# Eight node blocks instead of seven summed along gathered rows in each propagation step of a GNN kernel, with their stores issued by ScalarE

## The chip, the core and the metric

The kernel runs on one NeuronCore of a Trainium2 chip. Its engines are named as in the profile: PE (TensorE; PEld is its weight load), DVE (VectorE), ACT (ScalarE), POOL (GpSimd) and SP (SyncE, which only issues DMAs here). The metric is the device time of one execution in microseconds (us); lower is better. Each engine takes its instructions from its own queue in program order, and waits at the head of the queue for the semaphores that the next instruction names.

## The reference

Four graph layers act on 6250 nodes with 128 features (float32) and 100,000 edges that are sorted by destination. L0 is a mean over neighbours with two dense maps, a spectral filter, batch normalisation and GELU; L1 a relational convolution with 32 relations; L2 an attention layer with a feed-forward block. Before each, the nodes are layer-normalised, and each adds its result to `x`. The layer that matters here is the last one, ten steps of propagation over the same graph with self loops:

```python
src = jnp.concatenate([src, loop]); dst = jnp.concatenate([dst, loop])
norm = deg_inv_sqrt[src] * deg_inv_sqrt[dst]
def step(xk, _):
    msg = norm[:, None] * xk[src]
    agg = jax.ops.segment_sum(msg, dst, num_segments=n_nodes)
    return ((1.0 - ALPHA) * agg + ALPHA * h, None)
xK, _ = jax.lax.scan(step, x, None, length=K)          # K = 10
return jax.nn.relu(xK)
```

## The kernel before

The nodes are padded to 49 blocks of 128. With `z` the state scaled by the root of the degree, a step of L3 is a plain sum over neighbours, followed by one multiply and one add per node. The kernel gets that sum in two ways.

**By products.** For blocks 0 to `DW - 1` (42 of them) the adjacency matrix lies in DRAM as counts in fp8 (`adj`, built in L0 and L1 by `counted` and `put_matrix`; the self loop is put in too). `z` is kept in SBUF as two parts, a high and a low one, in `parts[step % 2]` (tiles `xr0` and `xr1`, type fp32r). A *group* is up to four destination blocks (`GD`): ten groups of four and one of two. A group's columns run over the 49 source blocks in *pieces* of seven source blocks (`GS`); the group of two has four pieces. A step so has 74 pieces (`NP`), and a piece goes through four hands:

- `load` (L1680): SP issues the DMA of the fp8 counts into `am` (six buffers).
- `cast` (L1691 on ACT, L1689 on DVE): the counts become fp32r in `ar` (three buffers). Every third piece is cast by DVE, the others by ACT. Piece n can be cast when piece n-3 is through PE.
- `product` (L1701, in two halves): for each source block and each part one matmul with the 128x128 part as weights and 512 columns of `ar` moving (256 in the group of two), summed in one PSUM bank.
- at a group's end `evict` (L1707, ACT) copies the sums to SBUF as `y`, `turn_back` (L1712, PE) transposes them, and `rows_behind` makes the new state: `scale` on DVE (L1626, L1631, L1632), `keep` on ACT (L1640, the high part), `store` on POOL (L1644, the new `z` to the table `z_at` in DRAM).

**By gathered rows.** For the last seven blocks (42 to 48) the edges are cut into 128 lanes of `LE` = 114 consecutive edges. `collect` has POOL gather, with one indirect DMA per list place (L694), the 128 rows of `z_at` that the lanes need at this place, `LC` = 6 places to a tile `rows3` (four buffers). `run_on` (L1003, DVE) adds along each lane, restarting where the destination changes; its first instruction reads the last row of the tile before. `put_down` (L1008) stores the running sums in the table `scan`; the lane ends go to `carried` (L1007). There are 19 such rounds in a step. Then `fetch_ends` gathers, for each of the seven blocks, a node's sum from `scan` and what the lane before it carried over, loads the node's own `z` row (`own`, through SP), and `add_up` (L1725, L1726, DVE) adds the three. `rows_behind` follows for these seven blocks too (`kind` "t", tail).

**The order.** All of this is put in one list, `plan`, with a time for each entry, in units of one piece; sorting it by time gives every engine's queue, and nothing is reordered afterwards. The last lines set it:

```python
pace, behind, late = 2.75, 6.2, 2
...
tiles, n = {}, step * NP + behind
for k in range(LE // LC):
    there = n + pace * (k + 1)
    then(there - pace, collect, rp, end3, k, z_at[step % 2], LC, tiles, "rows3")
    there = slot(there + late)
    then(there, run_on, end3, k, LC, tiles)
    there += 1.6
    then(there, put_down, nc.gpsimd.dma_start, end3, k, LC, tiles)
```

`slot` rounds a time up to the next multiple of three pieces (plus 0.01), which is just behind a cast of DVE's. So `scale` and `run_on` stand in DVE's queue behind such a cast, and `put_down` 1.6 pieces later in the queue of the engine that issues it. The steps follow each other without a barrier. A step first works on groups 0 and 1 over source blocks 0 to 34, because the last blocks of the state before come late.

Of the kernel before, what the change touches and what calls it, by code (L numbers as in the profile page):

```python
# [10 lines left out]
F32 = mybir.dt.float32  # L11
# [4 lines left out]
OP = mybir.AluOpType  # L16
# [5 lines left out]
D = 128  # L22
E = 100000
P = 125
# [49 lines left out]
F32R = mybir.dt.float32r  # L74
F8 = mybir.dt.float8e4
MULTI = 15
GD = 4
GS = 7
DW = 42
DW0 = 36  # L80
LE = 114
LE0 = 216
LC = 6
LC0 = 8
# [554 lines left out]
def _fast(ctx, tc, a, out, pre):  # L639
    nc = tc.nc  # L640
    TT, TS, STT = nc.vector.tensor_tensor, nc.vector.tensor_scalar, nc.vector.scalar_tensor_tensor
    ident, eps, deg = pre["ident"], pre["eps"], pre["deg"]
    P, W = FP, FW
# [16 lines left out]
    def nodes(table):  # L660
        return table.rearrange("(w p) d -> p w d", p=P)
# [53 lines left out]
    def list_end(name, w0, le):  # L715

        n = W - w0
        return dict(w0=w0, le=le, e0=E - LP * le, n=n, name=name,
                    src=const.tile([LP, le], I32, name=f"src_{name}"),
                    same=const.tile([LP, le], F32, name=f"same_{name}"),  # L720
                    end=const.tile([P, n], I32, name=f"end_{name}"),
                    carry=const.tile([P, n], I32, name=f"carry_{name}"),
                    scan=dram.tile([LP * le + 1, D], F32, name=f"scan_{name}"),
                    carried=dram.tile([LP + 1, D], F32, name=f"carried_{name}"))

    end0, end3 = list_end("e0", DW0, LE0), list_end("e3", DW, LE)

# [8 lines left out]
    z_at = [dram.tile([FN, D], F32, name=f"z_at{i}") for i in range(2)]  # L736
    z_first = dram.tile([FN, D], F32, name="z_first")
    h_rows = dram.tile([FN, D], F32, name="h_rows")

    adj = dram.tile([DW, P, W * P], F8, name="adj")  # L740

# [6 lines left out]
    late = l1_lists.enter_context(tc.tile_pool(name="flate1", bufs=1, side="right"))  # L748
# [13 lines left out]
    late = lists.enter_context(tc.tile_pool(name="flate", bufs=1))  # L762
# [12 lines left out]
                   allow_small_or_imprecise_dtypes=True)  # L775
    lane_sum = keyp.tile([CH, DW * GW // 4], F32, name="lane_sum")
    key_v = keyp.tile([CH, GB * 128], BF16, name="key_v")
# [13 lines left out]
    with tc.tile_pool(name="csr_k", bufs=1) as sp, tc.tile_pool(name="csr_kps", bufs=2, space=PSUM) as pp2:  # L791
# [9 lines left out]
        got = sp.tile([128, GB, CH], I32, name="p_got")  # L801
# [25 lines left out]
        for b0 in range(0, GB, 4):  # L827
            n = min(4, GB - b0)
# [218 lines left out]
    with tc.tile_pool(name="bxs", bufs=1) as bx, tc.tile_pool(name="bps", bufs=2, space=PSUM) as bps, \  # L1047
# [78 lines left out]
        tiles = {}  # L1126
# [20 lines left out]
        behind = None  # L1147
        for w in range(DW0 + 1):
# [15 lines left out]
            if w < DW0:  # L1164
                put_matrix(w, stag, bst)
                behind = stag
# [17 lines left out]
    with tc.tile_pool(name="fl1w", bufs=2) as wp, tc.tile_pool(name="fl1hr", bufs=3) as hp, \  # L1184
# [23 lines left out]
        def matrix_rest():  # L1208
            for w in range(DW0, DW):
                stag = bst.tile([P, W, P], F8, name="stag1")  # L1210
# [102 lines left out]
    own = l2p.tile([P, W, H], F32, name="own")  # L1313
# [9 lines left out]
    with tc.tile_pool(name="fl2w", bufs=2) as wp, tc.tile_pool(name="fl2ps", bufs=2, space=PSUM) as pp:  # L1323
# [5 lines left out]
        got, ht2 = {}, {}  # L1329
# [43 lines left out]
    with tc.tile_pool(name="fl2d", bufs=1) as l2d, tc.tile_pool(name="fl2r", bufs=4) as rp, \  # L1373
# [68 lines left out]
        state = None, None  # L1442
        for i in range(NT - FIRST, NT):
            rows = fetched(i)
            state = run(i, rows, *state)
# [11 lines left out]
        state = begin[:, SW:], begin[:, :SW]  # L1457
        for i in range(NT - FIRST):
            rows = fetched(i)
            state = run(i, rows, *state)  # L1460
# [8 lines left out]
        more = l2d.tile([LP, SW], F32, name="more2")  # L1469
# [14 lines left out]
    parts = [last.enter_context(tc.tile_pool(name="fl3x0", bufs=1)).tile([P, W, 2, D], F32R, name="xr0")]  # L1484
    with tc.tile_pool(name="fl2f", bufs=2) as fp, tc.tile_pool(name="fl2fps", bufs=1, space=PSUM) as pp, \
# [5 lines left out]
        got, fac, h1, ht3, ffs, us, z0 = ({} for _ in range(7))  # L1491
# [77 lines left out]
        def part5(b):  # L1569
# [23 lines left out]
    ap, cp, yp, sp, rp, ep = (last.enter_context(tc.tile_pool(name=f"fl3{k}", bufs=n))  # L1593
                              for k, n in (("a", 6), ("c", 3), ("y", 1), ("s", 2), ("r", 4), ("e", 1)))
# [7 lines left out]
    def then(time, do, *args):  # L1602
        plan.append((time, len(plan), do, args))

    def slot(time):

        return 3 * -int(-time // 3) + 0.01

    def rows_behind(time, step, w0, n, at):

        out_at, kind = step == K_STEPS - 1, "t" if w0 == DW else ""
        pool, wide = (ep, end3["n"]) if kind else (sp, GD)
        z_to, new = z_at[(step + 1) % 2], parts[(step + 1) % 2][:, w0:w0 + n]

        def fetch():
            at["first"] = pool.tile([P, wide, D], F32, name=f"first3{kind}")[:, :n, :]
            nc.sync.dma_start(at["first"], nodes(z_first)[:, w0:w0 + n, :])

        def fetch_kept():
            at["t"] = at["own"] if kind else pool.tile([P, wide, D], F32, name="split_t")[:, :n, :]  # L1620
            nc.sync.dma_start(at["t"], nodes(x_kept)[:, w0:w0 + n, :])

        def scale():
            z = at["z"] = at["more"] if kind else pool.tile([P, wide, D], F32, name="z3")[:, :n, :]
            for i in range(n):
                STT(z[:, i, :], at["sums"][:, i, :], d9[:, w0 + i:w0 + i + 1], at["first"][:, i, :],  # L1626
                    op0=OP.mult, op1=OP.add)
            if out_at:
                return
            at["t"] = at["own"] if kind else pool.tile([P, wide, D], F32, name="split_t")[:, :n, :]  # L1630
            TS(at["t"].bitcast(I32), z.bitcast(I32), -4096, None, op0=OP.bitwise_and)  # L1631
            TT(new[:, :, 1, :], z, at["t"], OP.subtract)  # L1632

        def keep():
            if out_at:
                for i in range(n):
                    nc.scalar.activation(at["z"][:, i, :], at["z"][:, i, :], AF.Relu,  # L1637
                                         scale=back[:, w0 + i:w0 + i + 1])
            else:
                nc.scalar.copy(new[:, :, 0, :], at["t"])  # L1640

        def store():
            if not out_at:
                nc.gpsimd.dma_start(nodes(z_to)[:, w0:w0 + n, :], at["z"])  # L1644
                return
            xb = at["t"]
            TT(xb, xb, at["z"], OP.add)  # L1647
            m = min(n, full - w0)
            nc.sync.dma_start(nodes(out[0:full * P, :])[:, w0:w0 + m, :], xb[:, :m, :])
            if m < n:  # L1650
                nc.sync.dma_start(out[full * P:N, :], xb[:tail, m, :])

        then(time - 6, fetch)
        if out_at and not kind:
            then(time - 1, fetch_kept)
        time = slot(time)
        then(time, scale)
        if out_at and kind:
            then(time + 0.05, fetch_kept)
        then(time + 2.3, keep)  # L1660
        then(slot(time + 2.4) if out_at else time + 2.7, store)

    groups = [(w, min(GD, DW - w)) for w in range(0, DW, GD)]
    cuts = [[W * i // n for i in range(n + 1)] for n in (W * nd // (GS * GD) + (W * nd % (GS * GD) > 0) for _, nd in groups)]
# [3 lines left out]
    loads, casts, sums = {}, {}, {}  # L1670
# [43 lines left out]
    def fetch_ends(step, at):  # L1714

        n = end3["n"]
        at["got"], at["more"], at["own"] = (ep.tile([P, n, D], F32, name=f"{k}3") for k in ("got", "more", "own"))
        nc.sync.dma_start(at["own"], nodes(z_at[step % 2])[:, DW:, :])
        for i in range(n):
            gather(at["more"][:, i, :], end3["carried"], end3["carry"], i)  # L1720
        for i in range(n):
            gather(at["got"][:, i, :], end3["scan"], end3["end"], i)

    def add_up(at):
        TT(at["more"], at["own"], at["more"], OP.add)  # L1725
        TT(at["got"], at["got"], at["more"], OP.add)  # L1726
        at["sums"] = at["got"]

    pace, behind, late = 2.75, 6.2, 2
    for step in range(K_STEPS):  # L1730
        for at, (g, c) in enumerate(order):
            n, key = step * NP + at, (step, g, c)
            then(n - 6.3, load, key)
            then(n - 2, cast, key, n)
            then(n, product, key, False)
            then(n + 0.45, product, key, True)
            if c == len(cuts[g]) - 2:
                state = {}
                then(n + 1, evict, g, state)
                then(n + 1.4, turn_back, g, state)  # L1740
                rows_behind(n + 1.75, step, *groups[g], state)
# [4 lines that stand above are left out]
            there = slot(there + late)  # L1746
            then(there, run_on, end3, k, LC, tiles)
            there += 1.6
            then(there, put_down, nc.gpsimd.dma_start, end3, k, LC, tiles)
        state = {}  # L1750
        then(there + 0.1, fetch_ends, step, state)
        there = slot(there + 6)
        then(there, add_up, state)
        rows_behind(there - 0.5, step, DW, end3["n"], state)
    with tc.manual_schedule():
        for _, _, do, args in sorted(plan, key=lambda p: p[:2]):
# [5 lines left out]
def gnn4_kernel(ctx: ExitStack, tc: tile.TileContext, a: dict, out: bass.AP):  # L1762
# [21 lines left out]
    with tc.tile_pool(name="csr", bufs=1) as sp, tc.tile_pool(name="csr2", bufs=4) as sp2, \  # L1784
# [89 lines left out]
        least = sp.tile([FW, 1], F32, name="p_least")  # L1874
        nc.gpsimd.memset(least, float(E - LP * LE) - 0.5)
        for w, e0 in ((DW, E - LP * LE0 - 0.5), (DW0, -1.0)):
# [72 lines left out]
```

## Time and profile before

| | us |
|---|---|
| median of three runs | 6846.81 (6821.8 to 6847.55) |
| the profiled execution's own time | 6823.96 |
| its span from first to last instruction | 6822.2 |
| L3, from the first product to the last | 3993 to 6808 |
| PE, DVE, ACT, POOL busy over the span | 3676.2, 3345.3, 2747.3, 3537.3 |
| PE, DVE, ACT, POOL busy in a mean step of L3 (of 281.5) | 252.6, 159.4, 167.6, 143.3 |

How to read it: the profile comes from one execution, so durations and sums are held against 6823.96. A PE record has its start and a modelled end, so matmuls overlap in it, and the distance between two starts says how fast PE is going. Gaps on an engine are put down to what released it. L3 is the stretch in which the change acts almost alone; its ten steps are counted from the last product of one to the last product of the next.

### The profile page before, as it was taken

To read this page: it belongs to the slowest core of one execution; us is meant where nothing else is said; L and a number is where in the kernel's file an instruction comes from. 1 tells how busy PE (TensorE), PEld (TensorE's weight loads), DVE (VectorE), ACT (ScalarE), POOL (GpSimd) and SP (SyncE) were. 2 spreads that over 40 slices of the span, in tenths; PEclk is the share of its full clock that TensorE was granted. 3 is DMA by queue.
4 is the path that set the end of the run, shared out by engine and by line. 5 is a ranking of instruction groups with operands and counts; after the bars stand their busy time and mean duration, and the time that the engine had idled before them with its cause. 6 is when DMAs were issued, how large, how long until landed. Compare 5 with 4: busy or idle time off the path is not lost. (4 is left out here: it accounts for less than half of the span.)

```text
span 6822.2 us, 55524 instructions
## 1 busy us (share of the span) xinstructions
PE 3676.2 (54%) x16892; PEld 2753.4 (40%) x16892; DVE 3345.3 (49%) x7571; ACT 2747.3 (40%) x3219; POOL 3537.3 (52%) x3583
## 2 busy tenths in 40 slices
PE   3655999700000020000000478799898998989998
PEld 3533654300000010000000157677776777767776
DVE  7454655422222224444545655556555565645655
ACT  0333655432222220000000565566565665656665
POOL 1265000177777756677676425446454554554644
PEclk8577999855555555555555799899998999989998
DMA  2233136632222213232222257677676776767766
GB/s 67 73 115 106 66 137 290 261 114 97 90 96 92 94 57 103 94 101 90 98 91 98 79 159 211 178 206 227 185 214 180 207 218 188 212 180 203 224 196 191
DMA packets 692861, 1003.89 MB, mean 147 GB/s; under 512 B 95753, under 2 KB 590738, under 8 KB 673094
## 3 DMA queue, kind: packets, MB, share of 16 engines
q1 hardware_dynamic: 546720, 677.59, 30.4%
q0 software_dynamic: 128304, 318.10, 16.1%
q10 hardware_dynamic: 17526, 4.56, 0.3%
q8 instruction: 134, 2.20, 0.1%
q14 instruction: 177, 1.45, 0.1%
HBM read 605.13 MB, written 397.87 MB: 147 GB/s over the span
## 5 line engine op out<-in xcount | busy, mean ns | idle before, releaser
L1701 PE MATMUL dense<-ar,xr 128*128 128x512 f32 (+1 forms) x10780 | 2495.7, 392 | 207.7 <-ACT ar L1691 89.1
L1701 PEld LDWEIGHTS dense<-ar,xr 128*128 128x128 f32 x10780 | 2015.0, 195 | 644.0 <-issue 124.5
L1691 ACT CAST ar<-am 128x3584 fp32r<-128x3584 fp8e4 (+1 forms) x494 | 1560.4, 3169 | 964.4 <-issue 385.3
L1689 DVE CAST ar<-am 128x3584 fp32r<-128x3584 fp8e4 (+1 forms) x246 | 933.8, 3796 | 1162.0 <-PE dense L1701 630.0
L694 POOL DMA_INDIRECT rows<-z_at,src_e x1140 | 1093.0, 959 | 667.5 <-issue 388.4
L694 POOL DMA_INDIRECT rows<-ftable,lane_src x782 | 833.2, 1065 | 366.0 <-issue 239.9
L694 POOL DMA_INDIRECT rows<-ftable,rel_l x782 | 830.4, 1062 | 245.2 <-issue 236.2
L1534 PE MATMUL ht_ps<-ident_p,h1g 128*128 128x128 f32 x49 | 10.3, 298 | 1270.4 <-ACT h1g L684 1270.1
L702 PE MATMUL ht_ps<-ident_p,long 128*128 128x128 f32 x49 | 16.0, 442 | 1129.3 <-ACT long L684 1125.8
L1282 ACT ACTIVATE rows<-rows,lane_norm 128x128 f32<-128x128 f32 x782 | 312.3, 401 | 766.3 <-issue 609.7
L1284 DVE SCALAR_TENSOR_TENSOR rows<-rows,same 128x128 f32<-128x128 f32 x733 | 257.8, 352 | 724.8 <-ACT rows L1282 610.4
L1534 PEld LDWEIGHTS ht_ps<-ident_p,h1g 128*128 128x128 f32 x49 | 6.6, 144 | 1279.9 <-ACT h1g L684 1275.2
L702 PEld LDWEIGHTS ht_ps<-ident_p,long 128*128 128x128 f32 x49 | 10.0, 208 | 1134.7 <-ACT long L684 1128.5
L1003 DVE SCALAR_TENSOR_TENSOR rows<-rows,same_e 128x128 f32<-128x128 f32 x1139 | 401.4, 352 | 44.4 <-issue 3.9
L1032 ACT ACTIVATE stag<-cnt_ps 128x784 fp8e4<-128x784 f32 x336 | 276.0, 823 | 340.5 <-remote 170.9
L1082 PE MATMUL dense<-xs,stag 128*128 128x384 bf16 x1764 | 356.8, 345 | 31.4 <-ACT stag L1032 25.2
L1225 PE MATMUL hr_ps<-fwr,ht 128*128 128x512 f32 x784 | 347.3, 597 | 1.5 <-ACT ht L704 1.5
L1437 DVE SCALAR_TENSOR_TENSOR rows<-rows,same 128x136 f32<-128x136 f32 x733 | 257.0, 351 | 170.3 <-remote 63.6
L1008 POOL DMA_DIRECT2D scan_e<-rows x190 | 110.3, 582 | 426.0 <-DVE rows L1003 424.5
L694 POOL DMA_INDIRECT rows<-h_rows,src_e x216 | 222.8, 1032 | 139.6 <-issue 78.6
L1014 DVE TENSOR_TENSOR hot_v<-key_v,iota_v 128x1568 bf16<-128x1568 bf16 x168 | 163.0, 970 | 224.2 <-remote 145.4
L1029 PE MATMUL cnt_ps<-hot_v,hot_s 128*128 128x196 bf16 x1344 | 183.2, 264 | 161.4 <-ACT stag L1032 130.3
(333 smaller groups left out, 3854.6 us busy)
## 6 DMA issues: line engine op xcount, KB each, us to landing
am<-adj SPq DMA_DIRECT2D x700, 448.0 KB
ftable<-hr SPq DMA_DIRECT2D x49, 2048.0 KB
scan_e<-rows POOLq DMA_DIRECT2D x190, 384.0 KB
scan<-rows SPq DMA_DIRECT2D x48, 1152.0 KB
scan<-rows SPq DMA_DIRECT2D x48, 1024.0 KB
adj<-stag SPq DMA_DIRECT2D x42, 784.0 KB
first<-z_first SPq DMA_DIRECT2D x100, 256.0 KB
z_at<-z POOLq DMA_DIRECT2D x90, 256.0 KB
```

The source lines that it names most:

```text
L694: nc.gpsimd.indirect_dma_start(out=tile_, out_offset=None, in_=table, in_offset=bass.IndirectOffsetOnAxis(ap=idx[:, k:k + 1], axis=0))
L1003: STT(tiles[k][:, t, :], prev, e["same"][:, col:col + 1], tiles[k][:, t, :], op0=OP.mult, op1=OP.add)
L1029: nc.tensor.matmul(ps[:, i, :HG], hot["s"][:, at // 2, :, at % 2], hot["v"][:, at // 2, :, at % 2], start=True, stop=True)
L1032: nc.scalar.activation(stag[:, :, at:at + 4 * GN].rearrange("p s (g d) -> p g s d", g=4), ps[:, :, :HG].rearrange("p g (s d) -> p g s d", ...
L1082: nc.tensor.matmul(ps, stag[:, s, :], xs[:, s].rearrange("p t d -> p (t d)"), start=(s == 0), stop=(s == W - 1))
L1225: nc.tensor.matmul(ps, ht1[b][:, i * P:(i + 1) * P], wr[:, 4 * q:4 * q + 4, :], start=True, stop=True)
L1282: nc.scalar.activation(rows[:, t, :], rows[:, t, :], AF.Copy, scale=norm_l[:, k:k + 1])
L1284: STT(rows[:, t, :], rows[:, t - 1, :] if t else before, same[:, k:k + 1], rows[:, t, :], op0=OP.mult, op1=OP.add)
L1437: STT(rows[:, t, :SW], rows[:, t - 1, :SW], same[:, k0 + t:k0 + t + 1], rows[:, t, :SW], op0=OP.mult, op1=OP.add)
L1689: nc.vector.tensor_copy(to, frm)
L1691: nc.scalar.copy(to, frm)
L1701: nc.tensor.matmul(sums[g][:, :nd * P], parts[step % 2][:, s, part, :], casts[key][:, i], start=(s == 0 and part == 0), stop=(s == W - 1 a ...
```

## The change

Four constants and a handful of lines differ. `DW` goes from 42 to 41, so eight blocks are summed along gathered rows, and the matrix `adj` has one block less, both where it is built (the six blocks built in L1 become five) and where it is used: the last group of a step has one block instead of two, two pieces instead of four, and matmuls of 128 columns instead of 256. `LE` goes from 114 to 132: 22 rounds of six gathers instead of 19, for which `pace` goes from 2.75 to 2.4. `put_down` is issued by `nc.scalar` instead of `nc.gpsimd`, at the same time in the plan. A node's own row is no longer loaded from `z_at`; `add_up` adds its two parts from SBUF instead, and stands 7 instead of 6 pieces behind. The tile `own` is gone, and its other two uses move to `got` (as `sums`) and, in the last step, to a buffer of `ar`.

```diff
-DW = 42
+DW = 41
 DW0 = 36
-LE = 114
+LE = 132
...
         def fetch_kept():
-            at["t"] = at["own"] if kind else pool.tile([P, wide, D], F32, name="split_t")[:, :n, :]
+            if kind:
+
+                at["t"] = cp.tile([P, GS * GD * P], F32R, name="ar").bitcast(F32)[:, :n * D].rearrange(
+                    "p (w d) -> p w d", d=D)
+            else:
+                at["t"] = pool.tile([P, wide, D], F32, name="split_t")[:, :n, :]
...
-            at["t"] = at["own"] if kind else pool.tile([P, wide, D], F32, name="split_t")[:, :n, :]
+            at["t"] = at["sums"] if kind else pool.tile([P, wide, D], F32, name="split_t")[:, :n, :]
...
-        at["got"], at["more"], at["own"] = (ep.tile([P, n, D], F32, name=f"{k}3") for k in ("got", "more", "own"))
-        nc.sync.dma_start(at["own"], nodes(z_at[step % 2])[:, DW:, :])
+        at["got"], at["more"] = (ep.tile([P, n, D], F32, name=f"{k}3") for k in ("got", "more"))
...
-    def add_up(at):
-        TT(at["more"], at["own"], at["more"], OP.add)
+    def add_up(step, at):
+        for part in range(2):
+            TT(at["more"], at["more"], parts[step % 2][:, DW:, part, :], OP.add)
         TT(at["got"], at["got"], at["more"], OP.add)
         at["sums"] = at["got"]
 
-    pace, behind, late = 2.75, 6.2, 2
+    pace, behind, late = 2.4, 6.2, 2
...
-            then(there, put_down, nc.gpsimd.dma_start, end3, k, LC, tiles)
+            then(there, put_down, nc.scalar.dma_start, end3, k, LC, tiles)
...
-        there = slot(there + 6)
-        then(there, add_up, state)
+        there = slot(there + 7)
+        then(there, add_up, step, state)
```

## The prediction

> **What bounds the kernel now.** I read the page's busy digits first, then L3 step by step, then what stops PE there.
>
> ```profile
> PE 3676.2 (54%) x16892; PEld 2753.4 (40%) x16892; DVE 3345.3 (49%) x7571; ACT 2747.3 (40%) x3219; POOL 3537.3 (52%) x3583
> ...
> PE   3655999700000020000000478799898998989998
> PEclk8577999855555555555555799899998999989998
> ```
>
> L3 is the last 41% of the span, and PE is its bound; no other engine passes 60% there. The timeline gives PE's undisturbed pace:
>
> ```profile
> 4258.28 0.60 PE L1712 MATMUL yt<-ident_p,y 128*128 128x128 f32 x4
> 4258.64 5.04 PE L1701 MATMUL dense<-ar,xr 128*128 128x256 f32 x40
> 4387.72 18.07 PE L1701 MATMUL dense<-ar,xr 128*128 128x512 f32 x79
> ```
>
> Less one matmul's length, 78 starts in 17.7 us are 0.227 us for 512 columns; likewise 0.12 for 256, and 0.11 for a transpose. A step then needs 980 x 0.227 + 98 x 0.12 + 42 x 0.11 = 239 us. It takes 281.5, so 43 us a step are lost. The stretches of one step show where (columns: PE, PEld, DVE, ACT, POOL busy, granted clock, DMA):
>
> ```profile
> 4289.00:4326.00 37.00, 21.74 (x88) 16.66 (x88) 8.30 (x3) 13.33 (x5) 22.68 (x24) 0.82 0.42 119
> 4326.00:4389.00 63.00, 63.00 (x279) 51.93 (x278) 44.00 (x65) 43.21 (x20) 22.75 (x26) 0.97 0.71 208
> 4389.00:4433.00 44.00, 27.20 (x113) 21.79 (x112) 15.35 (x23) 15.52 (x8) 31.87 (x35) 0.81 0.61 185
> 4433.00:4526.00 93.00, 91.70 (x411) 75.09 (x410) 67.75 (x97) 64.73 (x28) 49.96 (x58) 1.00 0.76 230
> 4526.00:4552.00 26.00, 19.53 (x95) 16.84 (x94) 11.58 (x17) 11.75 (x6) 14.09 (x15) 0.87 0.86 214
> 4576.00:4606.00 30.00, 23.05 (x91) 17.21 (x90) 11.08 (x3) 11.83 (x6) 17.12 (x18) 0.89 0.49 143
> ```
>
> POOL issues a gather every 1.25 us (0.95 busy, 0.30 between). In the first stretch it issues 24 without a break, and 37 us of PE hold 88 matmuls, worth 20 us: 17 lost. In the second the gathers come in sixes with pauses, and PE is busy for all of 63 us. The third has 30 gathers with only 0.6 us stores between sixes: about 19 lost. The fourth has sixes and twelves: about 1. The fifth is the step's 14 end gathers: about 5. The last is 18 in a row: 9 to 10. All L3 reads so: a *streak* of gathers costs its length less some 12 us (24 are 30 long, 18 are 22.5, 14 are 17.5), streaks up to 12 cost next to nothing, and a pause or another DMA issue in between takes much of the cost away. The streak comes first and PE stops inside it, so it isn't PE's halt that lets POOL run on. What joins the two the trace doesn't tell. DMA share falls in the lossy stretches, so it is not bandwidth.
>
> What breaks streaks today is POOL's own queue:
>
> ```profile
> POOL scan_e L1008 <- DVE rows L1003: 424.5, 53, 40.1
> POOL z_at L1644 <- DVE z L1626: 145.1, 17, 15.7
> POOL rows L694 <- DVE rows L1003: 82.6, 15, 7.6
> POOL rows L694 <- DMA scan_e<-rows: 67.3, 24, 6.5
> ```
>
> POOL stands 424 us before `put_down`, waiting for `run_on`: an in-order wait that costs PE nothing and spaces the gathers.
>
> **The change part by part, per step.**
>
> *PE.* 98 matmuls go from 256 to 128 columns. No row shows 128 moving fp32r columns. The nearest are 0.12 at 256 columns and 0.11 for the f32 transposes, which load 128x128 weights too; 0.227 is the far end. I take 0.115: 98 x 0.005 plus one transpose saves 0.6 us; the ends are 4 saved (if it halves with the columns to 0.08) and 10 lost. [...]
>
> *Casts and loads.* Two of 74 go: ACT loses 1.4 x 3.2 = 4.5 us, DVE 0.6 x 3.8 = 2.3, neither on the path. The load of `own` goes from SP, which has room.
>
> *DVE.* 18 more adds x 0.385 = 6.9 us; `add_up` three additions of 1024 elements instead of two of 896 (1.09 each): +1.6; an eighth column in `scale`. 159 becomes 167 of 280: covered by waits for PE.
>
> *ACT.* 23 stores. POOL takes 0.58 us for one; SP takes 0.32 for such a store of the L0 list: 7 to 13 us on an ACT that is busy 168 of 281. But each waits for `run_on`, and behind it in ACT's queue stands the next cast, for which PE waits. At an undisturbed slot DVE casts for 3.9 us and runs on for 2.3, done 6.2 us behind PE's release; ACT's own cast ends 6.4 behind it: no wait. A `scale` in between adds 2.5, a second `run_on` 2.3; PE, at 3.2 us a piece, wants the second ACT cast 12.9 us behind, so it may start at 9.7. One addition is just absorbed; both (11.1) make PE wait 2 us. With a pace of 2.4 and slots of 3, 22 rounds fall on 18 slots, four of them double; slots 15 (two scales) and 30 (scale and double) are too full: 4 us, 0 if DVE runs early, 10 if the single ones miss too.
>
> *POOL.* 18 + 2 more gathers: +25 us; 20 stores go: -12 busy, and with them the wait that spaced the gathers. What holds POOL now is the free tile alone: `collect` k needs the store of k-4, and `run_on` k-3, which reads that tile's last row. Six gathers take 7.5 us, and a round comes every 2.4 pieces of some 3.25 us = 7.8: POOL is as fast as the plan, with 0.3 us to spare and a `store` of 1.1 us every seven pieces. So the sixes join.
>
> I laid one step's plan on a time line, each queue in its order with these durations (all steps have the same phase now, 72 being a multiple of 3), PE stopped from 12 us into a streak until its end. Done so for the plan before, whose steps come in three phases, it gives 288, 284 and 270; the profile has 283 to 290, 287 to 290 and 268 to 273. At the start all four tiles are free and nothing stands between rounds 0 and 3: 24 gathers, as only every third step has now (the others 18). Then 6, 18, 12, 18 with a store inside, 6, 6, 18, 6, 18 with a store inside, and 16 at the end. Cost: 18 + 10.5 + 7.5 + 10.5 + 7 + 8 = 61.5, where the before column has 43. In the walk POOL is also late with its rows before several slots: `run_on` waits, DVE's next cast and ACT's behind its store are late, some 14 us, with ACT's 4 above 18 (bounds 0 and 25). The step is 238 + 61.5 + 18 = 317.5 against 281.5: +36.
>
> [...]
>
> *L1 and the end.* One block of `adj` less to build: 32 matmuls at 0.13 us (L1029) in a PE-bound stretch, -4 us once; bounds 0 and -8. The last step's `ar` buffer for `x_kept` changes nothing on the path.
>
> Sum on the profiled execution: 6824 + 360 - 4 = 7180; it lies 23 under the median, so 7203, say 7200.
>
> **The rivals.**
>
> *Faster: the pauses hold.* If tiles come free slot by slot (9.7 us) rather than at 7.8, each six is followed by 2 us of rest, and only the first 24 and the last 16 cost: 26 instead of 43, and PE's casts are in time: 238 + 26 + 5 = 269, -12 a step, 6723. Pauses of that size exist today between sixes, and the 63 us stretch is free of loss. Against it: 22 rounds on 18 slots leave no such rest. It decides where a release comes later than 9.5 us after the last.
>
> *Slower, but little.* Stops feed back: PE stopped, no tiles come free, and streaks end sooner than in my walk. Streaks 46 to 50, late casts 8 to 12: +10 to +20 a step, 6950 to 7040.
>
> *The narrow matmul is dear.* At 0.227 us, 10 us a step on top: about 7300. No row shows it, none excludes it.
>
> *That the change doesn't do what it says*: the lists' guard asks that block 41 starts behind edge 100000 - 16896; in these inputs it holds by 897 edges, so the same path runs.
>
> **How the numbers follow.** The walk's case 0.66 (7050 to 7400, its width from the late casts' 0 to 25 and streaks of 50 to 75), little slower 0.14, dear matmul 0.07, faster 0.09, no change 0.04. A change under 0.5% can hardly be told from none here. 6930 to 7420 leaves out the faster case, no change and the dear matmul's top, under 0.2. Chances: faster 0.09, same 0.04, slower 0.87.
>
> **What would show it.** Right: the steps all alike, near 317; POOL's wait for `run_on` at L1008 gone, and ACT with such a wait instead; stretches of 18 and more gathers with a clock near 0.8, at the start and several times within each step; POOL waiting at L694 for tiles. The narrow matmuls start 0.11 to 0.12 apart. Wrong: gathers in separated sixes and PE busy beside them; or streaks of 18 and PE busy beside them, which would end my law; or matmuls 0.2 apart in the last group.

## The result, and the profile after

The changed kernel takes 7297.12 us (median; 7289.56 to 7310.19) where the kernel before takes 6844.69 beside it: ratio 1.0673, interval 1.0647 to 1.07. The forecast of 7200 lies 1.3% below it, the range holds it. The profiled execution took 7304.2 us, 480 more than that of before, and 476 of these lie in L3, which runs from 3998 to 7289.

The page, with the same rows as shown of before:

```profile
PE 3827.4 (52%) x16850; PEld 2843.6 (39%) x16850; DVE 3396.4 (47%) x7750; ACT 2700.6 (37%) x3189; POOL 3600.8 (49%) x3583
...
PE   4657999100000200000007878878878787888887
...
PEclk8578999655555555555558989899988888898988
```

In L3 PE's digits are 7 and 8 where they were 8 and 9, and the clock shows the same dips. The steps are all alike now, 321 to 335 us, mean 330.2 (before: three phases, mean 281.8). The work of PE in a step is 237.5 us by the distances between its starts, so 93 us a step are lost, where it was 43.

POOL's and ACT's waits in L3 (engine, what waited, for what: us in total, times, longest):

```profile
POOL rows L694 <- DVE rows L1003: 754.5, 97, 51.8
POOL z_at L1649 <- DVE z L1631: 247.5, 26, 24.0
```
```profile
ACT ar L1696 <- DVE rows L1003: 225.8, 57, 7.1
```

The wait at L1008 is gone from POOL, which now waits at L694 for a free tile, and ACT's casts wait for `run_on`, as the prediction had it. One step in stretches, each from a streak's first gather to the next streak's first gather; a break of under 2 us does not end a streak here (columns: PE, PEld, DVE, ACT, POOL busy, granted clock, DMA):

```profile
4996.40:5053.60 57.20, 38.43 (x165) 31.20 (x164) 19.69 (x23) 23.27 (x9) 22.74 (x24) 0.85 0.45 131
5053.60:5095.20 41.60, 31.55 (x130) 24.91 (x129) 21.86 (x34) 20.53 (x9) 24.50 (x26) 0.92 0.60 191
5095.20:5118.50 23.30, 20.41 (x91) 16.24 (x90) 14.02 (x21) 13.65 (x6) 12.19 (x14) 1.00 0.68 211
5118.50:5152.00 33.50, 23.31 (x87) 17.83 (x86) 17.03 (x30) 13.64 (x6) 17.90 (x19) 0.87 0.58 181
```

These are streaks of 24, 24 (with two stores inside), 12 and 18 gathers. Counting PE's starts at their undisturbed distances, the stretches lose 21, 13, 4 and 15 us; the rest of this step (24 with 1.8 us between its two twelves, 12, 18 and 16) loses 13, 5, 11 and 11: 93 in all.

What a stop is can be read in the timeline of the first streak of another step (in brackets the engine's idle time and what ended it; `remote` is a semaphore's update for which the profile finds no instruction that ended just before):

```profile
4337.75 19.66 PE L1706 MATMUL dense<-ar,xr 128*128 128x512 f32 x86
...
4354.73 3.19 ACT L1696 CAST ar<-am 128x3584 fp32r<-128x3584 fp8e4 x1 [6.75 <-PE dense L1706]
...
4357.98 1.65 PE L1706 MATMUL dense<-ar,xr 128*128 128x512 f32 x6 [0.57 <-issue]
...
4369.29 0.94 POOL L694 DMA_INDIRECT rows<-z_at,src_e  x1 [0.30 <-issue]
4373.80 3.18 ACT L1696 CAST ar<-am 128x3584 fp32r<-128x3584 fp8e4 x1 [15.88 <-remote]
4374.57 3.89 DVE L1694 CAST ar<-am 128x3584 fp32r<-128x3584 fp8e4 x1 [22.76 <-remote]
...
4377.52 1.11 PE L1717 MATMUL yt<-ident_p,y 128*128 128x128 f32 x4 [17.89 <-ACT y L1712]
```

ACT's cast ends at 4357.92 and PE starts at 4357.98: ACT's release reaches PE at once. PE's releases don't: the next casts on ACT and DVE wait for pieces that PE had left by 4357.4, and start at 4373.8 and 4374.6, some 4 us behind the end of the streak's last gather (4370.2). Late loads of the counts are not the reason: the trace has them landed by 4342 for ACT's cast, and DVE's queue was past its wait for them at 4351.9, while the updates of PE's semaphore, for which both casts still wait, stand at 4373.73 and 4374.55. PE, ACT and DVE all stand; POOL alone goes on, a gather every 1.25 us. So PE stops because its own releases come late: the casts wait for them, `evict` stands behind a cast in ACT's queue, `turn_back` waits for `evict`, and PE's next products stand behind `turn_back`.

### The profile page after: what moved, and what is told of

The parts are those of the page before. It is cut to its first block, busy times and chain, and to the rows that moved or that the text cites. A ratio compares the mean times of both kernels' runs of the same rounds, so it can differ in the third digit from the quotient of the medians.

```text
span 7302.5 us, 56108 instructions
## 1 busy us (share of the span) xinstructions
PE 3827.4 (52%) x16850; PEld 2843.6 (39%) x16850; DVE 3396.4 (47%) x7750; ACT 2700.6 (37%) x3189; POOL 3600.8 (49%) x3583
## 5 line engine op out<-in xcount | busy, mean ns | idle before, releaser
L1706 PE MATMUL dense<-ar,xr 128*128 128x512 f32 (+1 forms) x10780 | 2637.0, 406 | 385.9 <-issue 179.0
L1706 PEld LDWEIGHTS dense<-ar,xr 128*128 128x128 f32 x10780 | 2107.4, 207 | 873.7 <-issue 249.0
L1696 ACT CAST ar<-am 128x3584 fp32r<-128x3584 fp8e4 x480 | 1524.7, 3179 | 1408.2 <-issue 418.7
L694 POOL DMA_INDIRECT rows<-z_at,src_e x1320 | 1254.4, 950 | 1248.2 <-DVE rows L1003 754.5
L1694 DVE CAST ar<-am 128x3584 fp32r<-128x3584 fp8e4 x240 | 912.0, 3800 | 1576.4 <-remote 795.8
L694 POOL DMA_INDIRECT rows<-ftable,lane_src x782 | 827.4, 1058 | 361.5 <-issue 238.0
L694 POOL DMA_INDIRECT rows<-ftable,rel_l x782 | 830.1, 1062 | 245.3 <-issue 237.6
L1003 DVE SCALAR_TENSOR_TENSOR rows<-rows,same_e 128x128 f32<-128x128 f32 x1289 | 454.5, 353 | 45.6 <-DMA rows<-h_rows,src_e 1.9
L694 POOL DMA_INDIRECT rows<-h_rows,src_e x216 | 223.0, 1032 | 136.8 <-issue 79.0
L694 POOL DMA_INDIRECT more<-carried_e,carry_e x93 | 95.6, 1028 | 286.6 <-DMA carried_e<-rows 261.6
```

Of the source, the lines that this page charges most:

```text
L694: nc.gpsimd.indirect_dma_start(out=tile_, out_offset=None, in_=table, in_offset=bass.IndirectOffsetOnAxis(ap=idx[:, k:k + 1], axis=0))
L1003: STT(tiles[k][:, t, :], prev, e["same"][:, col:col + 1], tiles[k][:, t, :], op0=OP.mult, op1=OP.add)
L1694: nc.vector.tensor_copy(to, frm)
L1696: nc.scalar.copy(to, frm)
L1706: nc.tensor.matmul(sums[g][:, :nd * P], parts[step % 2][:, s, part, :], casts[key][:, i], start=(s == 0 and part == 0), stop=(s == W - 1 a ...
```

## The experiments

The runs fell on chips of two kinds, so each is told with the time of the kernel before beside it. Chip A is that of the prediction (before: 6845 us). On B, D and E the kernel before took 6175, 6176 and 6170 us, on C 6762. Each chip was met in one session only, so what is called a kind of chip here may also be a state in which it was found. Ratios are against the kernel before on the same chip. "Lost" is a step's length less PE's own work in it.

**First group, chip B: one part undone, one part alone, and a pause.** `a_putpool` is the changed kernel with

```diff
-            then(there, put_down, nc.scalar.dma_start, end3, k, LC, tiles)
+            then(there, put_down, nc.gpsimd.dma_start, end3, k, LC, tiles)
```

and `b_putact` the kernel before with the opposite edit. `a_rest` and `b_rest` are the changed kernel and the kernel before with

```diff
+    def rest():
+        nc.gpsimd.iota(iota_s, pattern=[[1, FP], [0, 2]], base=0, channel_multiplier=0,
+                       allow_small_or_imprecise_dtypes=True)
...
             gather(at["more"][:, i, :], end3["carried"], end3["carry"], i)
+        rest()
...
             then(there - pace, collect, rp, end3, k, z_at[step % 2], LC, tiles, "rows3")
+            then(there - pace, rest)
```

> The changed kernel with one part undone: POOL issues put_down again, so its wait for run_on stands between the gathers once more; 41 blocks, 22 rounds, pace 2.4 and the own row from the parts stay. Streak theory (PE stops while POOL gathers on without a pause): the waits split only some of the streaks, since 22 rounds on 18 slots leave little rest: 315 to 320 us a step instead of 331, 7140 to 7190 us. Rival, ACT's queue (the casts behind put_down are what costs): nearly all of the 50 us a step comes back, 6850 to 6900. Rival, the extra round and blocks alone: 7300, nothing comes back.

> The kernel before with one part of the change alone: ACT issues put_down; 42 blocks, 19 rounds, pace 2.75. Streak theory: POOL no longer stands before put_down, sixes join to twelves and eighteens: 299 us a step instead of 281.5, about 7020 us, and POOL's wait for run_on at L1008 is gone. Rival, ACT's queue: the 20 stores a step with their waits delay the casts whatever POOL does: up to 330 a step, 7300. Rival, the extra round and blocks do it: 6850, no change.

> The changed kernel with a pause: behind every six gathers, and between the eight and eight end gathers, POOL writes the constant iota_s once more (1.5 us in its first execution, same values). That adds 23 x 1.8 = 41 us of POOL's time a step and takes no gather, cast or store away. Streak theory: no streak is longer than 8, so PE's stops go, 92 us a step today: 240 plus ACT's late casts of 5 to 20, but POOL needs 148 x 1.25 + 41 = 226 and its waits: 250 to 270 a step, 6490 to 6690 us. Rival, the gathers' total or their traffic is what stops PE, or POOL is simply late: 331 or more a step, 7300 to 7700.

> The kernel before with the same pause behind every six gathers and between the seven and seven end gathers: 20 x 1.8 = 36 us more on POOL a step. Streak theory: the 43 us a step that PE loses shrink to 5 to 10: 245 to 255 a step, 6480 to 6580 us, below both kernels. Rival: POOL's time is added to the rounds and nothing is won: 6850 to 7200.

| chip B, before 6174.79 us | us | ratio | us a step |
|---|---|---|---|
| a_putpool | 6546.21 | 1.0602 (1.0584 to 1.062) | 279.3 |
| b_putact | 6186.06 | 1.0019 (1.0009 to 1.0029) | 242.9 |
| a_rest | 6368.91 | 1.0314 (1.0297 to 1.0331) | 261.6 |
| b_rest | 6327.17 | 1.0248 (1.0231 to 1.0265) | 257.0 |

The four expectations reckoned with chip A's times, and on B their totals could not hold: PE doesn't stop there. (The step of `a_rest` came out as forecast, but without a stop to remove that shows nothing yet.) In `b_putact` POOL issues streaks of up to 36 gathers, and a streak of 24 costs 1.1 us on average (0.1 in nine of ten) instead of 16. With nothing for the pauses to save, they only cost: 15 us a step in the kernel before. And ACT's issuing of the stores by itself is nearly free, 1 us a step.

`a_putpool` was a miss of another kind: 30 us a step slower than the changed kernel proves to be on such a chip (below). Its waits, of POOL, DVE and PE over nine steps:

```profile
POOL rows L694 <- DMA scan_e<-rows: 194.2, 58, 7.6
```
```profile
DVE rows L1003 <- DMA rows<-z_at,src_e: 591.5, 372, 5.6
```
```profile
PE dense L1706 <- DVE ar L1694: 237.9, 96, 6.9
```

POOL, busy for 0.59 us with each store and then held up by a store's landing, can't fill tiles ahead. Its rows come after DVE's slot, DVE stands at `run_on` 66 us a step with its cast queued behind, and PE waits for that cast, 26 of the 42 us a step that it loses. So with 22 rounds on such a chip the stores cost more in POOL's queue than in ACT's.

**Second group, chip C: the two kernels again, and the pause.**

> The changed kernel unaltered, beside runs of the kernel before on the same chip. In the runs above, on another chip than that of the first profiles, the kernel before took 6175 instead of 6845 us, and streaks of 24 gathers cost PE 0.1 us there. Theory, two causes: PE's stops in long streaks depend on the chip, and the lateness of POOL's rows (run_on late, the casts behind it late) does not. Where the kernel before takes some 6175 us the change should then cost only the late casts, 5 to 25 us a step: ratio 1.01 to 1.04; where it takes some 6845, 1.067 again. Rival, one cause: the stops are all there is, then the ratio is 1.00 where there are none. Rival, the change costs the same everywhere: 1.06 to 1.07.

> The kernel before unaltered, for a trace of it on the same chip as the changed one: ratio 1.00. Where streaks of 24 gathers cost PE nothing its steps take 240 to 245 us, against PE's need of 239; where they cost 17 us, 281.

> The changed kernel with POOL's pause of 1.5 us behind every six gathers, once more. Where PE stops in long streaks (the kernel before near 6845 us) the pauses should take most of the stops away: about 265 us a step instead of 331, 6600 to 6700 us, faster than both; if they don't, the streaks' length is not what stops PE. Where it doesn't stop (6175) it is 262 a step again, 6370 us.

| chip C, before 6762.11 us | us | ratio | us a step | lost |
|---|---|---|---|---|
| after_again | 7179.78 | 1.0615 (1.0586 to 1.0645) | 317.9 | 80 |
| before_again | 6766.95 | 1.0004 (0.9988 to 1.0021) | 278.4 | 40 |
| a_rest_again | 6632.53 | 0.9811 (0.9783 to 0.9839) | 262.7 | 25 |

This is a chip like A, and here the pause is a test of the cause. It removes no gather, cast or store and puts POOL's gathers off by some 32 us a step (23 pauses of 1.4 us, by the lines below; 1.8 had been reckoned), and the step gets 55 us shorter. It is the same length as on chip B (262.7 and 261.6), where PE doesn't stop at all. One pause of POOL's:

```profile
5062.64 0.95 POOL L694 DMA_INDIRECT rows<-z_at,src_e  x1 [0.30 <-issue]
5063.61 1.53 POOL L1720 IOTA iota_s<- 128x256 bf16 x1
5065.31 0.96 POOL L694 DMA_INDIRECT rows<-z_at,src_e  x1 [0.17 <-issue]
```

The start streak of a step with the pauses, then that of the changed kernel on the same chip:

```profile
5056.30:5089.60 33.30, 33.30 (x152) 27.55 (x151) 16.98 (x16) 23.15 (x9) 26.65 (x27) 1.00 0.71 201
```
```profile
5282.40:5311.30 28.90, 18.60 (x81) 14.75 (x79) 5.71 (x2) 9.55 (x3) 21.85 (x23) 0.88 0.58 161
```

24 gathers in both: with 1.5 us behind every six PE is busy for the whole stretch, and 201 GB/s are moved beside it; without, it has 81 matmuls in 28.9 us. The kernel with pauses beats both kernels there, that of before by 1.9%. The pauses also lower the gathers' rate, from six in 7.5 us to six in 8.9; whether the unbroken length or the rate is what counts was not told apart.

**Third group, chip D: the best of both, and the change without stops.** `b_act_rest` is the kernel before with the edits of `b_putact` and `b_rest` together.

> The kernel before (42 blocks, 19 rounds, pace 2.75) with two edits: ACT issues put_down, and POOL pauses 1.5 us behind every six gathers and between the seven and seven end gathers. Theory of two causes (POOL's streaks, where the chip has them; POOL's rows coming late): POOL needs 128 x 1.25 + 20 x 1.8 + 12 = 208 us and waits only for free tiles, so neither acts: 243 to 252 a step on any chip, 6190 to 6250 us where the kernel before takes 6175 and 6430 to 6520 where it takes 6760 to 6845. Rival, pauses cost whatever they save (they made the kernel before 15 us a step slower where it had no stops): 257 a step, 6330 or 6550.

> The kernel before with ACT issuing put_down and nothing else, once more. Where the kernel before takes some 6760 or more: without the waits at L1008 the sixes join, and the streaks theory gives 299 us a step against 281, ratio 1.02 to 1.04; rival, ACT's issuing is harmless everywhere, 1.00. Where it takes some 6175: 1.00 to 1.01 by both.

> The changed kernel unaltered, as the yardstick of the two others on this chip. Where the kernel before takes some 6760 or more: 318 to 331 us a step, ratio 1.06 to 1.07. Where it takes some 6175, only the late casts are left, which the pauses laid bare as 25 us a step: 250 to 265 a step, ratio 1.01 to 1.035.

| chip D, before 6175.89 us | us | ratio | us a step | lost |
|---|---|---|---|---|
| b_act_rest | 6208.70 | 1.0054 (1.0037 to 1.0071) | 245.1 | 7 |
| b_putact_again | 6185.51 | 1.0015 (1.0005 to 1.0024) | 242.9 | 5 |
| after_third | 6244.52 | 1.0111 (1.009 to 1.0131) | 249.2 | 12 |

On a chip without stops the change costs 1.1%, not 6 to 7%, and a step loses 12 us, not the 25 that were expected of the late casts. Its first two streaks of a step there, of 24 and of 108 gathers:

```profile
4755.30:4792.90 37.60, 37.60 (x171) 31.14 (x170) 21.06 (x23) 23.31 (x9) 22.75 (x25) 1.00 0.70 196
4792.90:4937.00 144.10, 138.00 (x617) 113.02 (x617) 106.18 (x164) 96.46 (x42) 109.49 (x116) 1.00 0.84 259
```

POOL gathers for 144 us with no pause of over 2 us, and PE loses 7 us in them, at full clock. PE's waits are short ones for casts and for `evict`, 8 of the 12 us that a step loses (sums over nine steps):

```profile
PE dense L1706 <- ACT ar L1696: 28.2, 17, 1.8
PE yt L1717 <- ACT y L1712: 27.7, 20, 3.3
PE dense L1706 <- DVE ar L1694: 16.5, 9, 1.8
```

The longest is 3.3 us; on chip A the longest wait at `turn_back` was 18.5.

**Fourth group, chip E.** The same two kernels on one more chip, again one without stops.

> The kernel before with ACT issuing put_down and POOL's pause of 1.5 us behind every six gathers, once more. Where the kernel before takes 6175 us: 245 us a step and 6209 us again. Where it takes 6760 or more, PE's stops should be gone with the streaks: 245 to 252 a step, 6430 to 6520 us, ratio 0.95 to 0.965, faster than both kernels. Rival there, pauses of 1.5 us do not clear streaks that come without the store's wait: 270 or more a step, ratio 0.99 or above.

> The kernel before with ACT issuing put_down and nothing else. Where the kernel before takes 6175 us: 243 us a step, ratio 1.002 again. Where it takes 6760 or more: the streaks (24, 12, 36, 12, 18, 12 and 14 gathers a step in the traces without stops) are no longer broken by the waits at L1008: 299 us a step by the streak theory, ratio 1.02 to 1.04, and the pauses of the kernel beside it take it all back. Rival: 281, ratio 1.00, if it is not the joining of the sixes that costs.

`b_act_rest_again` took 6205.03 us (ratio 1.0046, 1.0029 to 1.0063; 245.1 a step), `b_putact_third` 6182.54 (1.002, 1.001 to 1.0029; 243.0 a step), beside 6169.80 of the kernel before. Both repeat chip D. What the two do where PE stops stays open: that ACT's issuing alone costs 17 us a step there, and that `b_act_rest` would be the fastest kernel there (some 33 us a step less than the kernel before, if the pauses bring its step to 245 as they brought that of `a_rest` to one length on B and C), was not shown. The two show something else: where ACT issues the stores, the pauses cost the kernel before 2 us a step (245.1 against 242.9), not the 15 of `b_rest`.

Is it something else that differs between the chips? Not the casts: ACT's takes 3.19 us and DVE's 3.89 on A and on D. But POOL's gathers do differ, long before L3. POOL's gathers of L1 between 1700 and 2200 us, on A in the changed kernel, then on D (count, busy, mean ns of one, idle):

```profile
L694 POOL DMA_INDIRECT rows<-ftable,rel_l x357 | 391.2, 1096 | 108.8 <-issue 108.8
```
```profile
L694 POOL DMA_INDIRECT rows<-ftable,rel_l x400 | 378.3, 946 | 121.9 <-issue 112.4 <-DMA rows<-ftable,rel_l 7.0 <-DVE rows L1284 2.4
```

On A a gather takes 0.945 us there at first and 1.096 from some 1550 us on; on C it takes 1.095 in the same stretch (`before_again`), on D 0.946. So the slower gather was seen on the two chips on which PE stops, and the faster one on one of those on which it doesn't. In L3 the means are alike: 0.95 to 0.96 us from 4400 to 6100 us, on A and on B.

## Why the prediction was right, step by step

**The mechanism held, on this kind of chip.** Long streaks of gathers stop PE, and the change lengthens them: the pauses of `a_rest_again` show it as a cause, not only as a coincidence in the trace. (That it is not bandwidth rests on the pauses too, 201 against 161 GB/s; the DMA share falls in three of the four stretches of before that lose most, but the end gathers' has 0.86.) What the prediction did not know is that this depends on the chip and not on the program alone: on three chips of five the same streaks cost next to nothing. The result came from a chip with stops, like the profile that the forecast was made from; on D the change costs 1.1%, far below the forecast's range.

**The sum was 36 us a step, it is 48; the split was wrong in both terms.** Streaks: 61.5 was forecast for the changed kernel. On A the step loses 93, of which 12 are lost on chip D too, so the stops are some 81 (on C 80 - 12 = 68), an estimate that takes these 12 to be the same on all chips. Late casts: 18 was forecast as an addition. On D all that is lost is 12, and the change adds 7 a step by the times (6244.5 - 6175.9 over ten steps). So the streaks' term was too small by 20, and that of the casts too large by 11 (18 against 7); the errors partly cancelled, and that the total came within 1.3% is in part luck. (The 3 us that are left of the difference: of the 43 that the kernel before loses some 4 are not stops either, by `b_putact_again`.) The streaks were mis-sized twice: the second streak of a step is 24 gathers, not 6 and then 18 behind a pause, and a streak costs a little more than its length less 12 (24 at the start: 21, not 18; 18: 12 on average, not 10.5; 12: 3, not 0; the 16 at the end 14, not 8, for the reason told below).

**ACT.** Its waits for `run_on` came (57, of 4 us on average, in the ten steps), and its issuing alone costs 1 us a step on three chips without stops, within the bounds of 0 to 10. POOL was rightly seen to be free of the wait; that this freedom is worth 30 us a step where nothing stops PE (279 against 249) was not in the sum.

**PE's narrow matmuls.** The middle distance between two starts in the last group is 0.111 us on D: the 0.115 that was taken held. The 0.08 of the prediction's saving end was shown by no run, and half of the 0.12 at 256 columns would be 0.06; where the granted clock was 1.00, the starts were 0.112 apart on A too. But on A 64% of these distances are over 0.2 us, and the group takes 23.4 us a step instead of 11.2; in the kernel before the group of two takes 16.1. A distance of 0.2 in the last group was one of the prediction's signs of being wrong. The lines show why it came, the longest run of the group's matmuls on D, then on A, and A's stretch:

```profile
4971.70 9.90 PE L1706 MATMUL dense<-ar,xr 128*128 128x128 f32 x80
```
```profile
4638.09 11.77 PE L1706 MATMUL dense<-ar,xr 128*128 128x128 f32 x48 [1.43 <-issue]
```
```profile
4638.00:4650.00 12.00, 11.89 (x50) 11.21 (x50) 2.77 (x1) 3.44 (x2) 0.00 (x0) 0.50 0.21 61
```

PE is busy throughout, POOL is done, and the granted clock is 0.50. In this step it was 1.00 in the 18 us ahead of the group (4611 to 4629), 0.79 from 4629.4 to 4638, where PE stops again and again beside the last end gathers, and 0.50 from there to 4650. Over all ten steps the narrow matmuls of A start 0.213 us apart (middle) where the clock is 0.50 and 0.112 where it is 1.00; on D the stretch with the group in it (4937 to 4986) has 1.00. So the rival of the dear matmul had its price (10 us) nearly right for A and its reason wrong: not the shape, but the lower clock that follows the stop. Against a forecast of -0.6 this is +7 a step, and it stands within the 81 above.

**L1** did not get 4 us shorter: on D, L3's first product starts at 3735.5 us in the changed kernel and at 3735.2 in `b_putact_again`.

**The rivals.** That the pauses hold came out false: tiles came free early enough for streaks of 24 on A, and of 108 on D. "Slower, but little", 1.5 to 3% on A, was not it either; on the chips without stops it is 1.1%, and there it was short waits for casts and `evict`, with no stops that could feed back.

## What to carry to other kernels

An in-order wait that looks like pure loss can be spacing something out: before moving it away, look at what its engine will do with the freedom, and whether a short pause (1.5 us behind six gathers here) keeps the spacing at a known price: where it wasn't needed, 15 us a step in the kernel before, 12 in the changed one, and 2 where the stores were out of POOL's queue in the kernel before. A law read from one chip's trace is a law of that chip until another has shown it: the same edit cost 6.7, 6.2 and 1.1% on three of them, and the fastest kernel that was run on one kind (`a_rest`) is 3% slower than the kernel before on the other. When a wait is moved from one queue to another, count what it held back as well as what it now blocks.

## What was not expected of the hardware

- Two kinds of chips: the kernel before takes 6762 to 6845 us on two and 6170 to 6176 on three. In L3 that is 278 to 282 against some 242 us a step (an estimate from the 243 of `b_putact` and the times), some 4 us above PE's own need of 239 on the second kind; the stages ahead of L3 take 3993 and 3998 us on A and some 3735 on D.
- On the first kind a release from PE to ACT and DVE reaches them late during a long streak of POOL's gathers (16 us in the streak shown on A; on C the wait of `turn_back` for `evict`, which such a late release drew out on A, took up to 18.0 in the changed kernel), while a release from ACT to PE takes 0.06 us. What joins POOL's gathers to PE's releases no run here shows; the amount of data doesn't, for with pauses more bytes move in the same stretch (201 against 161 GB/s). Nor do the gathers pile up: in the first streak shown the last packet of a gather ends 1.1 to 2.5 us behind its issue on A.
- A pause of 1.5 us in which POOL writes 128x256 numbers is enough behind six gathers (7.5 us) to keep the four such groups of the stretch shown free of any loss; in a later stretch of the same step (5187.9 to 5221 us) PE was busy for only 29.7 of 33.1 us, at a clock of 0.90.
